# A transformer block with 576 features: 64x64 tiles for the last 64 features of every projection, with biases moved off TensorE

## The chip, the cores and the metric

The kernel runs on one core of a Trainium2 chip. The metric is the device time of one execution in microseconds (us). All data is fp32.

## The reference, cut to what matters

Two batches of 2048 tokens with C = 576 features go through one conditioned transformer block: 16 heads of D = 36 features, and an MLP with FF = 2304.

```python
ada = silu(c) @ W_ada + b_ada          # six vectors of 576 for each batch
h = layernorm(x) * (1 + scale_msa) + shift_msa
qkv = h @ W_qkv + b_qkv                # 576 -> 1728
o = softmax((q * D**-0.5) @ k.T) @ v   # for each head
x = x + gate_msa * (o @ W_proj + b_proj)
h = layernorm(x) * (1 + scale_mlp) + shift_mlp
x = x + gate_mlp * (gelu(h @ W_fc1 + b_fc1) @ W_fc2 + b_fc2)
```

## The kernel before, in words

A projection sums over 576 features in KC = 5 chunks: four of P = 128 partitions and one of KL = 64. In the last chunk a 65th row holds the bias in the weights and a one in the activations, so the bias is added by the matmul. Only the first layer of the MLP (`up_to`, lines 990 to 1047) differs: it takes the last 64 features of two column blocks together, in four matmuls of 64x64 (`last`, line 992, matmul line 998; a "quad" below), with features held twice, in partitions 0 to 63 and 64 to 127. Its bias is added by ACT (line 1023).

*Front* (lines 159 to 484). For four token blocks of QB = 512 of batch 0, `queries_keys_values` normalises, turns (L218) and modulates tokens (L136, L138) and computes queries and keys (L233, nine column blocks m) and values (L258, four tiles of tokens, two halves of C2 = 288 columns). The results go to DRAM (`qk_d`, `v_d`). Beside this, `later` computes the conditioning (`rows_of`, L331, into PSUM cleared by `cleared`, L313) and multiplies W_proj and W_fc2 by their gates (`gated`). Two PSUM pools serve: three `wide` tiles of two banks, and two single `bank`s.

*Main part* (from line 487). There are 128 units, 8 blocks of 512 queries times 16 heads. Each unit has NG = 4 groups, and one pass of the loop over G handles, in the order of the code: scores of a later group on PE (L538, 36x64 tiles) and their copy by ACT (L551); a step of other work from `fill`; exponentials by ACT (L597); at a unit's first group the turn of the maxima (`turn`, L574); the last part of the fill step (`lasts`); values weighted by exponentials (`weigh`, L609, 64x64 tiles); running maxima (L556) and the subtraction of the maximum (L593) on DVE; then `take`, which copies a unit's sum out of PSUM (L621, L622); then `flush`, which runs what an earlier step put into `later`; then the second half of the fill step, `dones`, which empties its PSUM; and `advance`, which moves the loads of the next item by one step.

The fill steps are generators. First come queries, keys and values of batch 1 (`projections`, L812 and L774), then for each finished block k an item `[gather(k), block(k), k]`. `gather` loads the block's sums and outputs, inverts the sums, and multiplies (L867 to L901); the reciprocals go through DRAM (`rec_d`, stored from POOL, and loaded by 20 DMAs on SP). `block` calls `begin` for the output projection (po, L929), the residual and the statistics, then runs the MLP: pf (L1012, L998), gelu on ACT and DVE, py (L1062), in three parts (`down`). A block's last part runs behind `begin` of the next block, when that is ready.

The order is set by a planner written out by hand: each step yields a cost, `RATE` is credited in each pass, and a step runs in each even pass, and in an odd one when the credit is above `RATE`. Odd passes otherwise turn two pieces of normalised tokens (`lights`, L719). POOL's queue carries weights, x, `gather`'s loads and the accumulating stores of the second half of each head (L630); SP's carries keys, values, the maxima (`m_d`, L585 and L588) and `r`. Each of these queues is worked in program order, so a DMA that waits holds those behind it. What remains behind the loop (the end of block 6 and all of block 7's MLP) runs without attention beside it, and `room` then takes PSUM from two pools.

Of the kernel before, what the change touches and what calls it, by code (L numbers as in the profile page):

```python
# [22 lines left out]
def dit_block_kernel(  # L23
# [51 lines left out]
    wpr_d = [scratch.tile([C + 1, C], F32, name=f"wpr_d{b}") for b in range(B)]  # L75
    w2_d = [scratch.tile([FF, C], F32, name=f"w2_d{b}") for b in range(B)]
    gb_d = [scratch.tile([C], F32, name=f"gb_d{b}") for b in range(B)]
    NB = B * NQB
# [12 lines left out]


    mod = const.tile([P, 4, KC, B], F32, name="mod")
    nc.vector.memset(mod, 0.0)
    nc.vector.memset(mod[KL : KL + 1, 0:2, KC - 1, :], 1.0)
    b1 = const.tile([P, NF], F32, name="b1")
# [59 lines left out]
    with ExitStack() as front:  # L156
# [32 lines left out]
        def queries_keys_values(b, tb):  # L189
# [11 lines left out]
            for i in range(TB):  # L201
                xn = lnp.tile([P, CP], F32, tag="xn", name=f"xn_{b}_{tb}_{i}", bufs=6)
                seq(nc.vector.memset(xn[:, C:CP], 0.0))
                seq(
                    nc.vector.tensor_scalar(
                        xn[:, 0:C], xts[i], rs[:, i : i + 1], nm[:, i : i + 1],
                        op0=ALU.mult, op1=ALU.add,
                    )
                )
                xns.append(xn)  # L210
# [4 lines left out]
            def turn(kc):  # L215
                pt = bank(f"pt_{b}_{tb}_{kc}")
                for i in range(TB):
                    seq(nc.tensor.transpose(pt[:, ts(i, P)], xns[i][:, ts(kc, P)], ident))  # L218
                return pt

            pts = []
            if (b, tb) == (0, 0):
                pts = [turn(kc) for kc in range(2)]
                yield
# [4 lines left out]
            for m in range(2 * C // P):  # L229
                pq = bank(f"pq_{b}_{tb}_{m}")  # L230
                for kc in range(KC):
                    seq(
                        nc.tensor.matmul(  # L233
                            pq,
                            lhsT=w_in[: rows(kc), kc, ts(m, P)],
                            rhs=hT[: rows(kc), kc, :],
                            start=(kc == 0),
                            stop=(kc == KC - 1),
                        )
                    )  # L240
                ev = evp.tile([P, QB], F32, tag="ev", name=f"ev_{b}_{tb}_{m}")
                if m < C // P:
                    seq(nc.scalar.mul(ev, pq, SCALE))
                elif m == C // P:
                    seq(nc.vector.tensor_scalar_mul(ev, pq, qscale))
                else:
                    seq(nc.vector.tensor_copy(ev, pq))
                seq(nc.sync.dma_start(out=qk_d[b][ts(m, P), ts(tb, QB)], in_=ev))
                if m == 2 * C // P - 1 and tb == NQB - 1:
                    first_keys.extend(load_keys(0))  # L250
                yield
            for i in range(TB):
                t = tb * TB + i
                pv = wide(f"pv_{b}_{t}")
                for n in range(2):
                    for kc in range(KC):
                        seq(
                            nc.tensor.matmul(  # L258
                                pv[:, n, :C2],
                                lhsT=hT[: rows(kc), kc, ts(i, P)],  # L260
                                rhs=w_in[: rows(kc), kc, ds(2 * C + n * C2, C2)],
                                start=(kc == 0),
                                stop=(kc == KC - 1),
                            )
                        )
                vt = evp.tile([P, H, HA], F32, tag="vt", name=f"vt_{b}_{t}", bufs=3)
                seq(nc.vector.memset(vt[:, :, 0:1], 1.0))
                to = vt.rearrange("p (n h) e -> p n h e", n=2)
                for n in range(2):
                    src = pv[:, n, :C2].rearrange("p (h d) -> p h d", d=D)  # L270
                    if i % 2:
                        seq(nc.scalar.copy(to[:, n, :, 1:HA], src))
                    else:
                        seq(nc.vector.tensor_copy(to[:, n, :, 1:HA], src))
# [4 lines left out]
        hTs = {}  # L279
        stages = [queries_keys_values(0, tb) for tb in range(NQB)] + [queries_keys_values(1, 0)]  # L280
# [5 lines left out]
        def load_in(n):  # L286
# [4 lines left out]
            seq(nc.sync.dma_start(out=to[0:KL, KC - 1, :], in_=last[:, cols]))  # L291
            seq(nc.sync.dma_start(out=to[KL : KL + 1, KC - 1, :], in_=b_qkv[cols].unsqueeze(0)))

        load_in(0)
        load_in(1)
        next(stages[1])
        load_in(2)

# [23 lines left out]
        seq(nc.vector.tensor_copy(cT.rearrange("p k b -> p (k b)"), pt[:, 0 : KC * B]))  # L322
        def rows_of(part):
# [19 lines left out]
        def modulation(part, t):  # L343

            pm = wide(f"pm_{part}")[:, 0, :]
# [9 lines left out]
            spans = [(0, P, 0, KC - 1), (0, KL, KC - 1, KC)]  # L355
            if part // 3:
                spans.append((64, KL, KC - 1, KC))
# [59 lines left out]
        def later():  # L417
# [5 lines left out]
            yield  # L423
            yield
            g1 = []
            yield from gates(2, g1)
            was[3] = load_ada(3)
            g2 = []
# [3 lines left out]
            for b in range(B):  # L432
                seq(nc.vector.tensor_scalar_mul(half[b], g2[b], 0.5))
                r = ap.tile([1, C], F32, name=f"b2_{b}")
                seq(nc.gpsimd.dma_start(out=r, in_=b_fc2.unsqueeze(0)))
                seq(nc.vector.tensor_mul(r, r, g2[b][0:1, :]))
                seq(nc.gpsimd.dma_start(out=gb_d[b].unsqueeze(0), in_=r))
# [7 lines left out]
                for i, job in enumerate(split(w_proj))  # L445
            ]
            jobs.append(
                (
                    b_proj.unsqueeze(0).unsqueeze(1), 1, 1, g1,
                    [wpr_d[b][C : C + 1].unsqueeze(1) for b in range(B)],  # L450
                )
            )
# [6 lines left out]
            for part in (3, 4):  # L459
                t = rows_of(part)  # L460
                yield
                modulation(part, t)
# [21 lines left out]
        seq(nc.gpsimd.dma_start(out=b1, in_=b_fc1.rearrange("(f p) -> p f", p=P)))  # L484
# [4 lines left out]
    with ExitStack() as main_part:  # L489
# [144 lines left out]
        state = {"wpr": None, "turn": 0}  # L634
# [15 lines left out]
        def load_cols(key, w, bias, lo, n):  # L650

            t = mp.tile([P, KC, 2 * P], F32, tag="w1", name=f"w1_{key}_{lo}")
            main, last = pieces(w)
            cols = ds(lo, n)
            seq(nc.gpsimd.dma_start(out=t[:, 0 : KC - 1, :n], in_=main[:, :, cols]))
            seq(nc.gpsimd.dma_start(out=t[0:KL, KC - 1, :n], in_=last[:, cols]))
            seq(
                nc.gpsimd.dma_start(out=t[KL : KL + 1, KC - 1, :n], in_=bias[cols].unsqueeze(0))
            )
            return t  # L660

        def load_square(key, src):

            if state["wpr"] is None or state["wpr"][0] != key:
                t = bp.tile([P, KC, C], F32, tag="wpr", name=f"wpr_{key}", bufs=1)
                rest, bias = src
                main = rest[0 : (KC - 1) * P].rearrange("(kc p) n -> p kc n", p=P)
                seq(nc.gpsimd.dma_start(out=t[:, 0 : KC - 1, :], in_=main))
                seq(nc.gpsimd.dma_start(out=t[0:KL, KC - 1, :], in_=rest[(KC - 1) * P : C]))
                seq(nc.gpsimd.dma_start(out=t[KL : KL + 1, KC - 1, :], in_=bias))  # L670
# [3 lines left out]
        def load_x(key, b, qb):  # L674
            xs = []
            for i in range(TB):
                t = bp.tile([P, C], F32, tag="x2", name=f"x2_{key}_{i}", bufs=8)
                seq(nc.gpsimd.dma_start(out=t, in_=x[b, ts(qb * TB + i, P), :]))
                xs.append(t)
            return xs  # L680

        def normed(key, xs, mvs, twice=False):
# [4 lines left out]
            def make(lo, hi):  # L687
                rs, nm = by
                for i in range(lo, hi):
                    xn = xp.tile([P, CP], F32, tag="xn", name=f"xn_{key}_{i}")  # L690
                    spans = [(0, 0, C)]
                    if twice:
                        spans.append((C, C - KL, KL))
                    else:
                        seq(nc.vector.memset(xn[:, C:CP], 0.0))
                    for to, at, n in spans:
# [8 lines left out]
            half = TB // 2  # L705
            return xns, [
                lambda: by.extend(rstd_of(bp, mvs, key)),
# [26 lines left out]
        made = {}  # L734

# [16 lines left out]
        def projections(b, tb):  # L752

            key = f"q{b}_{tb}"
            wv = load_square("v", (w_qkv[:, 2 * C :], b_qkv[2 * C :].unsqueeze(0)))
            pairs = [(m, min(2, 2 * C // P - m)) for m in range(0, 2 * C // P, 2)]
            ws = {m: load_cols(key, w_qkv, b_qkv, m * P, n * P) for m, n in pairs[:2]}
# [11 lines left out]
            def values(i):  # L769
                pv = room(f"pv_{key}_{i}")  # L770
                for n in range(2):
                    for kc in range(KC):
                        seq(
                            nc.tensor.matmul(  # L774
                                pv[n][:, :C2],
                                lhsT=hT[: rows(kc), kc, ts(i, P)],
                                rhs=wv[: rows(kc), kc, ts(n, C2)],
                                start=(kc == 0),
                                stop=(kc == KC - 1),
                            )  # L780
# [489 lines left out]
```

## Time and profile before

| | us |
|---|---|
| median of 3 runs | 3801.6 (3800.6 to 3804.5) |
| the profiled execution | 3804.53, its span 3802.8 |
| granted TensorE clock | 0.995 of full speed |
| front, to the first scores | 296.4 |
| main loop | 296.4 to about 3547 |
| behind the loop | from about 3547 |
| DMA | 362.6 MB, 95 GB/s over the span |

In the rows that follow, a row of the timeline has the start, the length, the engine and line, and how many records were merged; in square brackets stands the idle time before it and who ended it. A row of the waits has the engine and what it ran, after the arrow what it waited for, the sum, how often, and the longest. "PEld" is the weight load of PE.

### The profile page before, as it was taken

The page shows a single profiled execution, that of the slowest core. Times are in us where ns is not written, and L with a number is a line of the kernel's source. Part 1 is how long each engine was busy: PE and PEld are TensorE (multiplying, and loading weights), DVE is VectorE, ACT ScalarE, POOL GpSimd, SP SyncE. Part 2 cuts the span into 40 slices and gives each one's busy share as a digit, 9 for nine tenths or more (in the row PEclk, how much of TensorE's full clock was granted, in tenths as well). Part 3 has the DMA queues.
Part 4 walks back from the last instruction along what each step waited for, and adds up shares of the span by engine and source line. Part 5 has one row for each costly group of instructions (what it writes and reads, how often), then busy time and mean ns, then how long its engine had stood idle before and what let it go on. Part 6 is the DMA issues. An engine that isn't in the chain of part 4 may idle for free.

```text
span 3802.8 us, 58130 instructions
## 1 busy us (share of the span) xinstructions
PE 3748.3 (99%) x23429; PEld 1762.1 (46%) x23429; DVE 2946.1 (77%) x2995; ACT 2335.5 (61%) x2196; POOL 564.7 (15%) x814
## 2 busy tenths in 40 slices
PE   8999999999999999999999999999999999999998
PEld 4554343444344544444444544453444444444555
DVE  4525778788888888888889888888889888988422
ACT  0005667766866676667676677667666766776321
POOL 0201112111111021101111111012110211111111
PEclk9999999999999999999999999999999999999999
DMA  6722434344434344434343433434342444343321
GB/s 218 270 99 76 97 78 108 86 122 96 93 81 98 59 103 86 102 55 103 69 95 89 105 77 83 96 62 112 81 99 57 107 83 97 70 95 79 87 84 56
DMA packets 415986, 362.58 MB, mean 95 GB/s; under 512 B 312731, under 2 KB 312731, under 8 KB 415718
## 3 DMA queue, kind: packets, MB, share of 16 engines
q1 hardware_dynamic: 352662, 177.06, 23.5%
q0 software_dynamic: 61328, 178.27, 15.4%
q8 instruction: 185, 3.03, 0.4%
q10 hardware_dynamic: 1728, 3.54, 0.3%
q14 instruction: 83, 0.68, 0.1%
HBM read 287.52 MB, written 71.21 MB: 94 GB/s over the span
## 4 chain that ended last, share of the span: by engine, by line
PE 93%; issue 4%; DVE 1%; ACT 1%; DMA 1%; POOL 0%; POOLq 0%; SPq 0%; ACTq 0%; DVEq 0%
PE av L609 23%; PE s L538 23%; PE py L1062 13%; PE pf L1012 13%; PE pq_q L812 4%; PE pq L233 4%; PE po L929 4%; PE pv_q L774 2%; PE pf L998 2%; PE pv L258 2%; PE mt L574 2%; PE pa L331 0%; PE pt_b L719 0%; ACT e L551 0%; DMA o_d<-up 0%
## 5 line engine op out<-in xcount | busy, mean ns | idle before, releaser
L551 ACT COPY e<-s 128x1024 f32<-128x1024 f32 x1024 | 989.6, 1024 | 684.4 <-PE s L538 680.2
L593 DVE TENSOR_TENSOR e<-e,m 128x2048 f32<-128x2048 f32 x512 | 1161.6, 2274 | 3.2 <-DMA m<-m_d 3.2
L556 DVE TENSOR_TENSOR acc<-acc,e 128x1024 f32<-128x1024 f32 x768 | 938.9, 1222 | 197.6 <-ACT e L551 155.0
L597 ACT ACTIVATE e<-e 128x2048 f32<-128x2048 f32 x512 | 991.6, 1937 | 1.2 <-DVE e L593 1.1
L609 PE MATMUL av<-e,v 64*64 64x512 f32 x8192 | 981.7, 594 | 0.0
L538 PE MATMUL s<-qT,kT 36*64 36x512 f32 x8192 | 975.7, 590 | 3.1 <-ACT e L551 2.3
L1062 PE MATMUL py<-w,gT 128*128 128x288 f32 x2304 | 583.5, 411 | 5.2 <-DVE gT L1042 3.5
L538 PEld LDWEIGHTS s<-qT,kT 36*64 36x64 f32 x8192 | 310.2, 133 | 563.8 <-issue 517.5
L1012 PE MATMUL pf<-h_b,w_b 128*128 128x512 f32 x1152 | 533.6, 607 | 4.4 <-DMA w_b<-in_L_cond_W_fc_dram 4.3
L609 PEld LDWEIGHTS av<-e,v 64*64 64x64 f32 x8192 | 291.8, 133 | 518.3 <-issue 478.5
L1062 PEld LDWEIGHTS py<-w,gT 128*128 128x128 f32 x2304 | 433.3, 191 | 183.7 <-issue 40.0
L630 POOL DMA_DIRECT2D o_d<-up x128 | 109.8, 858 | 2091.1 <-DMA o_d<-up 1117.4
L1012 PEld LDWEIGHTS pf<-h_b,w_b 128*128 128x128 f32 x1152 | 208.9, 190 | 324.6 <-issue 312.0
L584 DVE TENSOR_REDUCE mx<-mt 128x4 f32<-128x512 f32 x128 | 88.2, 689 | 197.3 <-PE mt L574 196.8
L1023 ACT ACTIVATE gT<-pf,b 128x512 f32<-128x512 f32 x144 | 99.0, 688 | 191.3 <-PE pf L998 136.6
L1034 DVE SCALAR_TENSOR_TENSOR th<-th,gT 128x1024 f32<-128x1024 f32 x72 | 88.0, 1222 | 104.0 <-ACT th L1032 104.0
L929 PE MATMUL po<-wpr_p,oT 128*128 128x288 f32 (+1 forms) x640 | 163.0, 410 | 0.1
L556 DVE TENSOR_TENSOR acc<-e 128x1024 f32<-128x1024 f32 x128 | 155.4, 1214 | 9.2 <-ACT e L551 9.2
L233 PE MATMUL pq<-hT,w_in 128*128 128x512 f32 (+1 forms) x360 | 158.6, 597 | 0.3 <-ACT hT L136 0.2
L1074 DVE TENSOR_TENSOR x_b<-py,x_b 128x288 f32<-128x288 f32 x192 | 81.4, 451 | 93.0 <-PE py L1062 93.0
L929 PEld LDWEIGHTS po<-wpr_p,oT 128*128 128x128 f32 (+1 forms) x640 | 119.2, 190 | 54.2 <-issue 11.0
L631 POOL DMA_DIRECT2D sum_d<-up x128 | 143.6, 1122 | 0.0
(142 smaller groups left out, 2275.1 us busy)
## 6 DMA issues: line engine op xcount, KB each, us to landing
w<-w_d POOLq DMA_DIRECT2D x72, 576.0 KB, 5.9
v<-v_d SPq DMA_DIRECT2D x128, 296.0 KB
kT<-qk_d SPq DMA_DIRECT2D x256, 144.0 KB
w_b<-in_L_cond_W_fc_dram POOLq DMA_DIRECT2D x72, 512.0 KB, 4.6
m<-m_d SPq DMA_DIRECT2D x128, 256.0 KB
qT<-qk_d SPq DMA_DIRECT2D x256, 72.0 KB
w_d<-wg POOLq DMA_DIRECT2D x12, 864.0 KB, 4.9
qk_d<-ev SPq DMA_DIRECT2D x36, 256.0 KB
```

Source lines behind the costliest of these rows:

```text
L233: nc.tensor.matmul(pq, lhsT=w_in[: rows(kc), kc, ts(m, P)], rhs=hT[: rows(kc), kc, :], start=(kc == 0), stop=(kc == KC - 1),)
L538: nc.tensor.matmul(s[ts(c, 64), i, :], lhsT=self.kT[at, ds((2 * g + j) * P + 64 * c, 64)], rhs=self.qT[at, :], start=True, stop=True,)
L551: seq(nc.scalar.copy(self.es[g][:, j], s))
L556: top = lambda out, x, y: seq(nc.vector.tensor_max(out, x, y))
L593: seq(nc.vector.tensor_sub(e, e, m))
L597: seq(nc.scalar.activation(e, e, AF.Exp))
L609: nc.tensor.matmul(self.av[ts(i, 64), r, :], lhsT=self.v[ts(r, 64), ds((c + i * (HALF // P)) * HA, 64)], rhs=e[ts(r, 64), j, i, :], start= ...
L631: seq(nc.gpsimd.dma_start(out=sums, in_=hi[0:1, :], accum_op=ALU.add))
L812: nc.tensor.matmul(pq, lhsT=w[: rows(kc), kc, ts(j, P)], rhs=hT[: rows(kc), kc, :], start=(kc == 0), stop=(kc == KC - 1),)
L929: nc.tensor.matmul(po[n][:, :C2], lhsT=oT[: rows(kc), kc, ts(i, P)], rhs=wpr[: rows(kc), kc, ts(n, C2)], start=(kc == 0), stop=(kc == KC - 1),
L1012: nc.tensor.matmul(pfs[j], lhsT=w1[:, kc, ts(j, P)], rhs=h2[:, kc, :], start=(kc == 0 and j == 0), stop=(kc == KC - 2 and j == 1),)
L1062: nc.tensor.matmul(py[n][:, :C2], lhsT=gTs[f - f % 2][:, f % 2, ts(i, P)], rhs=w2s[f - f % 2][:, f % 2, ts(n, C2)], start=(j == 0), stop=( ...
```

## The change

- All projections take the last 64 features in quads. The tails of weights and activations are held twice; ones and bias rows go.
- Biases: queries, keys and the MLP's first layer get theirs when ACT or DVE empties PSUM, from a tile `bias`, which is loaded by rows and transposed on PE. Values get theirs in an addition on DVE (before: copies by ACT, in the front half of them by DVE). The gated bias of the output projection is added by loading it as a broadcast into the residual's tiles and accumulating x on top by DMA; that of the second layer by four accumulating DMAs, in place of a load and four additions on DVE.
- `gather` loads the residuals (before: `begin`). The first weights of an item are loaded in the item in front (`early`).
- In the loop `take` runs behind `dones`; the first half of xn is put off by a pass when the statistics came in the same one; costs, `RATE` (2.55 to 2.51) and the first credit (-10 to -32) are new.
- In the front, PSUM for the conditioning is cleared a step earlier, the first block's five transposes run together, queries and keys use `wide`.
- The very last part of block 7 runs its first two tiles together, all but the last two chunks first; its stores go out in halves from SP.

```diff
+    def quads(outs, lefts, rights, starts):
+        for r in range(2):
+            for c in range(2):
+                seq(
+                    nc.tensor.matmul(
+                        outs[r][ts(c, 64), :],
+                        lhsT=lefts[r][:, ts(c, 64)],
+                        rhs=rights[r],
+                        start=starts[r],
+                        stop=not starts[r],
+                    )
+                )
+    def halves(t, kc):
+        return [t[ts(r, 64), kc, :] for r in range(2)]
...
             pts = []
             if (b, tb) == (0, 0):
+                spare = [wide(f"pt_{i}") for i in range(2)]
                 pts = [turn(kc) for kc in range(2)]
+                pts += [turn(2 + n, spare[0][:, n, :]) for n in range(2)]
+                pts.append(turn(4, spare[1][:, 0, :]))
...
+            for m in range(0, NQK, 2):
+                pq = wide(f"pq_{b}_{tb}_{m}")
...
+                    if two and r == 0:
+                        quads(
+                            [pq[:, i, :] for i in range(2)],
+                            [w_in[ts(i, 64), KC - 1, ts(m + i, P)] for i in range(2)],
+                            tail,
+                            (False, True),
+                        )
...
+                if i % 2 == 0:
+                    rest_of(i, pvs[0])
+                    rest_of(i + 1, pvs[1])
...
+    def by_square(outs, src, t, i):
+        w_, tail = square(t)
+        for n in range(2):
+            for kc in range(KC - 1):
+                seq(
+                    nc.tensor.matmul(
+                        outs[n][:, :C2],
+                        lhsT=src[:, kc, ts(i, P)],
+                        rhs=w_[:, kc, ts(n, C2)],
+                        start=(kc == 0),
+                        stop=False,
+                    )
+                )
+        return lambda: quads(
+            [o[:, :C2] for o in outs],
+            [half[:, ts(i, P)] for half in halves(src, KC - 1)],
+            tail,
+            (False, False),
+        )
-        def load_x(key, b, qb):
+        def load_x(key, b, qb, bias=None):
             xs = []
             for i in range(TB):
                 t = bp.tile([P, C], F32, tag="x2", name=f"x2_{key}_{i}", bufs=8)
-                seq(nc.gpsimd.dma_start(out=t, in_=x[b, ts(qb * TB + i, P), :]))
+                if bias is not None:
+                    seq(nc.gpsimd.dma_start(out=t, in_=bias.partition_broadcast(P)))
                 xs.append(t)
+            how = {} if bias is None else {"accum_op": ALU.add}
+            for i, t in enumerate(xs):
+                seq(nc.gpsimd.dma_start(out=t, in_=x[b, ts(qb * TB + i, P), :], **how))
             return xs
...
             for i in range(TB):
                 yield values(i)
+                to = f"q{b}_{tb + 1}"
+                if i == 0:
+                    early[to] = first_cols(to)
...
-            seq(nc.gpsimd.dma_start(out=oT[0:KL, KC - 1, :], in_=o_d[k][(KC - 1) * P : C]))
-            seq(nc.gpsimd.memset(oT[KL : KL + 1, KC - 1, :], 1.0))
+            for half in halves(oT, KC - 1):
+                seq(nc.gpsimd.dma_start(out=half, in_=o_d[k][(KC - 1) * P : C]))
+            b, qb = divmod(k, NQB)
+            loaded[k] = load_x(f"b{k}", b, qb, gp_d[b])
             yield
             yield
             seq(nc.vector.reciprocal(sums, sums))
...
-            gb = xp.tile([P, CP], F32, tag="xn", name=f"gb_{k}")[:, :C]
-            seq(nc.gpsimd.dma_start(out=gb, in_=gb_d[b].partition_broadcast(P)))
-            extra = [
-                lambda i=i: seq(nc.vector.tensor_add(x2s[i], x2s[i], gb)) for i in range(TB)
-            ]
+            for t in x2s:
+                seq(
+                    nc.gpsimd.dma_start(
+                        out=t, in_=gb_d[b].partition_broadcast(P), accum_op=ALU.add
+                    )
+                )
...
+                early[k + 1] = {f: load_w1(k + 1, f) for f in (0, 2)}
                 yield from begin(k + 1)
...
-                    if f is not None:
+                    if f is None:
+                        return
+                    if state["norm"] == state["slot"]:
+                        later.append(f)
+                    else:
                         f()
...
+                    for lo, hi in ((0, per - 2), (per - 2, per)):
+                        for i in range(at):
+                            weigh(i, pys[i], lo, hi)
+                    yield 11.88, lambda: [add(i, pys[i]) for i in range(at)]
...
-            if 0 <= G < NU * NG and g == NG - 1:
-                units[u].take()
             flush()
             for done in dones:
                 done()
+            if 0 <= G < NU * NG and g == NG - 1:
+                units[u].take()
             advance()
```

## The prediction

> **What bounds the kernel now.** I read the page's table of engines and the chain that ended last first:
>
> ```profile
> PE 3748.3 (99%) x23429; PEld 1762.1 (46%) x23429; DVE 2946.1 (77%) x2995; ACT 2335.5 (61%) x2196; POOL 564.7 (15%) x814
> PE 93%; issue 4%; DVE 1%; ACT 1%; DMA 1%; POOL 0%; POOLq 0%; SPq 0%; ACTq 0%; DVEq 0%
> ```
>
> PE's busy time alone proves little, because pipelined matmuls overlap, but the chain says the same: 93% of what set the end is PE. A matmul taken off PE should therefore shorten the kernel by its own time. Next come PE's waits, the only other time to be won:
>
> ```profile
> PE pq_q L812 <- DMA w_q<-in_L_cond_W_qkv_dram: 7.3, 1, 7.3
> PE pf L1012 <- DMA w_b<-in_L_cond_W_fc_dram: 4.3, 1, 4.3
> PE pa L331 <- issue: 4.3, 3, 1.6
> PE py L1062 <- DVE gT L1042: 3.5, 1, 3.5
> PE s L538 <- ACT e L551: 2.3, 1, 2.3
> PE py L1062 <- DVE x_b L1074: 1.6, 1, 1.6
> ```
>
> Last, PE's timeline, for prices. Each fp32 matmul is two records there (x10 is five matmuls). In the main loop, in the front, and behind the loop:
>
> ```profile
> 437.20 4.56 PE L812 MATMUL pq_q<-h_q,w_q 128*128 128x512 f32 x10
> 449.20 4.56 PE L812 MATMUL pq_q<-h_q,w_q 128*128 128x512 f32 x10
> ...
> 596.62 4.56 PE L812 MATMUL pq_q<-h_q,w_q 128*128 128x512 f32 x10
> 608.14 4.56 PE L812 MATMUL pq_q<-h_q,w_q 128*128 128x512 f32 x10
> ...
> 2310.44 3.70 PE L1012 MATMUL pf<-h_b,w_b 128*128 128x512 f32 x8
> 2322.43 3.70 PE L1012 MATMUL pf<-h_b,w_b 128*128 128x512 f32 x8
> 2333.10 3.70 PE L1012 MATMUL pf<-h_b,w_b 128*128 128x512 f32 x8
> ```
> ```profile
> 97.02 30.23 PE L233 MATMUL pq<-hT,w_in 128*128 128x512 f32 x70
> ```
> ```profile
> 3651.48 1.09 PE L998 MATMUL pf<-h_b,w_b 64*64 64x512 f32 x8
> 3652.50 7.13 PE L1012 MATMUL pf<-h_b,w_b 128*128 128x512 f32 x16
> 3659.56 1.09 PE L998 MATMUL pf<-h_b,w_b 64*64 64x512 f32 x8
> ```
>
> Full 512-column matmuls in a row cost 30.08/35 = 0.8595 us each (start to start); 288-column ones 19.43/40 = 0.4858 (line 258, x80). 512 against 288 gives 1.67 ns a column and no fixed part, so 256 columns cost 0.432.
>
> **Part 1: the tails leave PE.** pf (lines 1012 and 998) already has the new form, so it prices it.
> - *In the loop* two steps of queries/keys, with one turn of maxima between them, take 12.00 + 11.52 = 23.52 us. Two steps of pf, with one turn, take 11.99 + 10.67 = 22.66. The difference, 0.86, is two tail matmuls against one quad beside the 64x64 av tiles. So a quad costs 0.86 there, the array's ideal, and 0.485 at 288 columns.
> - *Between full tiles* (behind the loop) quad plus eight full matmuls repeat every 3659.56 - 3651.48 = 8.08 us, of which eight times 0.8595 is 6.88. A quad costs 1.20, or 0.86 plus 0.34 for going into small tiles and back.
>
> The Trainium skill speaks against small tiles here: "TensorEngine Tiling (Array Packing)", section "Tiling Modes", says that a change of tiling mode drains the array. The row in the loop shows no added drain, because av changes the mode there anyway; the row behind the loop does. Were the drain paid at all 64 new quads of the loop too, 64 x 0.34 = 22 us of the gain below would go. I take each row in its place.
>
> Sums. Loop, 4 token blocks: 16 pairs x 0.86 = 13.8; four single column blocks, where four times 0.86 + 0.86 becomes eight half matmuls + half a quad, save 0.43 each = 1.7; 16 value tiles and 28 output projections (blocks 0 to 6) lose two 288-column tails and gain one 288 quad: 44 x 0.485 = 21.3. Together 36.8. Front, 4 blocks, with the drain: pair 2 x 0.86 - 1.20 = 0.515, times 4; single 0.07; values, two quads per two tiles under one drain, 4 x 0.486 - 0.97 - 0.34 = 0.63, times 2: 3.4 a block, 13.6. Behind the loop, 4 output projections x 0.14 = 0.6. **PE: -51.0.**
>
> **Part 2: the waits.**
> - w_q at 422.79: weights of the next item are loaded during its predecessor's values. 7.30 of idle goes, and the stretched group (7.45 against 4.56) gives 2.9 more: -10.2. Next late would be the turned h_q, whose last transposes ended at 410, before PE went idle at 415.5: nothing.
> - w_b at 3644.98: the same, 4.34 + (6.57 - 3.70) = -7.2. Next late is h_b: transposes end at 3640.6, evictions take 0.78 each on ACT, and the first four are needed one by one at 0.86; no new wait.
> - py at 3772.9 waits 3.53 for the last gelu. The two tiles' first four matmuls per half (16 x 0.486 = 7.8 us) now come first and cover it: -3.5.
> - At 1715 scores wait 2.27 for ACT, which had been given the new xn right behind the statistics of the same step; the groups there stretch by 1.8 and 1.5 more. Deferring xn to the next step removes it: -5.5.
> - At 3190 py waits 1.57 for its banks: DVE freed them only after `take`, which sat idle for av. With `take` behind the evictions: -1.6. The price: the sum's copies are later, by evictions of 0.8 to 1.9 us, and the next unit's first av matmul queues behind them; there PE has 1.7 of scores and 3.5 to 6 of a step to do first. Nothing.
> - pa's three waits (1.54, 1.61, 1.19): PSUM is cleared a step earlier, -4.3. Banks of pq in front of transposes (0.8, DVE ev L247): -0.8, because pq moves to the wide buffers.
> - Start: all five transposes move ahead of the modulation matmuls (12 x 0.135 = 1.6 later mod) and save as much behind them: nothing. Bias transposes and their three DVE operations lie under the 6.2 us that PE is idle before pa at 11.36. Last store: halves from SP, perhaps -0.5.
>
> I worked the planner's credit through with both sets of costs: both give 24 steps in odd slots and both leave the loop at the same step (pf 13 of block 6), so nothing moves from loop to tail. Sum of waits: **-33.6**, and I allow **+4** for new ones (steps fall into other odd slots; values are freed by DVE before turned transposes).
>
> **Part 3: what is added elsewhere.** Values go from ACT (402 ns a half) to DVE (449 ns as a copy, 451 for an add from PSUM, line 1074). In the loop that is 32 x 0.45 = 14 us more DVE, but the gb additions, 32 x 0.751 = 24 us, leave it. The skill's "TensorEngine Tiling", section "Performance Considerations", would have both engines empty PSUM once tiles speed PE up. By it values on DVE alone are a step back; were each of the 16 in the loop late by its two adds, 0.9 us, 14 us would go. The row says 39.5 of 54 us of DVE are busy in the value stage at 531, so I take nothing; the evicted bank is already waited for by 0.55 from ACT.
> POOL: `gather` now issues two tails, four broadcasts of the bias and four accumulating loads of x ahead of the store of the reciprocals; four accumulating gb loads follow `lit`, and the first add that needs those is eight steps away. SP gets two more loads of 0.4 us per block. What is queued behind POOL's wait is the rival below. Early w1 loads wait for the same two buffers at most one step; then only stores of o_d follow them. ACT's bias operand costs 688 against 597 ns, 36 times, off the path.
>
> **Sum.** 3804.5 profiled - 51.0 - 33.6 + 4 = 3723.9. The median is 2.9 below the profiled run: **3721 us**.
>
> **Rivals.**
> *A, as summed* (0.74): 3704 (no drain in front: -10; no new waits: -4; and a little at the start) to 3738 (half the waits come back).
> *B, the waits only change place* (0.12): the last three groups, or w_q and w_b, are followed by others as long. Then PE's 51 remain and some 5 of waits: 3746. For: PE at 99% leaves other engines little slack. Against: each wait has a named cause that the edit takes away, with nothing late behind it.
> *C, quads of 288 or 256 columns run at the price of 512* (0.08): four weight loads (133 ns each by line 538's PEld row) might bound them. 64 + 20 such quads x 0.375 = 31 lost: 3750. Against: the 310 us of PEld busy for 8192 loads are 38 ns each, 152 per four, under the 243 ns of one pass of 288.
> *D, slower: the bias row ahead of the reciprocals* (0.06).
>
> ```profile
> gb<-gb_d POOLq DMA_DIRECT2D x8, 288.0 KB, 6.5
> ```
> ```profile
> 1168.06 0.57 POOL L881 DMA_DIRECT2D rec_d<-sums  x1 [0.42 <-DVE sums L880]
> 1172.37 1.96 SPq L892 DMA_DIRECT2D r<-rec_d  x4
> 1178.39 0.35 SPq L585 DMA_DIRECT2D m_d<-mx  x1
> ```
>
> An accumulating load must wait on POOL until its broadcast has landed (nearest row: 6.5 us for one). Issues of 0.8, the 6.5 and four of 1.08 put the reciprocals' store at about 1178.5 instead of 1168.1; r follows at 1182.5 on SP, and the next unit's maxima m_d, behind it on SP, slip by 6 us. m would land near 1190.4, and the subtraction that needs it runs at 1191.7; exponentials are a further step away, so some 5 us are spare. Each us beyond that stops PE, in each of seven blocks. If the four together need 6.5, nothing; the other end, four in series (26 us), is 19 later, 14 beyond the slack: 7 x 14 = 98, and 3819. It becomes slower than before when the broadcasts take over about 23 us. The 1024 KB of oT land in 6.1, so I take the short end. Partly so: 3757. Behind the loop the same delay meets 14.5 us of slack (oT done 3580.8, po at 3595.3).
>
> **How the numbers follow.** A 0.74, B 0.12, C 0.08, D 0.06. 3704 to 3750 holds A, B and most of C, some 0.85. A measurement of this kernel can tell 0.2%, 8 us, from no change; only D reaches that: faster 0.95, same 0.01, slower 0.04.
>
> **What would show it.** Right: PE busy near 3700 or less; no w_q, w_b or gT row in PE's waits; two steps of queries/keys in 22.66; an output projection's step 0.49 shorter; m_d rows behind r at each block, with no wait of DVE for m. Wrong: line 593 waiting for m beyond the 3.2 us of before (D); PE groups of 288 quads over 0.6 (C); new PE waits on DVE for values, or on ACT e (B).

## The result, and the profile after

The changed kernel takes 3772.4 us (median of 6 runs, 3765.4 to 3775.8) where the kernel before takes 3802.2: a ratio of 0.9919 (95% interval 0.9906 to 0.9931). It is faster, as forecast, but by 30 us instead of 81, and outside the range. Its profiled run is its fastest, 3765.4 with a span of 3763.6, so the trace shows less of the loss than the median has. Beside the experiments the kernel before took 3803.5 to 3805.4, so differences to the changed kernel are good to some 3 us.

The engines on the page after:

```profile
PE 3706.8 (98%) x23926; PEld 1727.1 (46%) x23926; DVE 2950.2 (78%) x3002; ACT 2331.1 (62%) x2164; POOL 617.1 (16%) x868
```

PE's busy time fell by 41.5 us and the span by 39.2, so PE idles no less than before (56.8 us, where it was 54.5). The largest new waits of PE are these:

```profile
PE s L625 <- DMA qT<-qk_d: 10.7, 5, 5.0
PE pq L277 <- ACT ev L261: 6.9, 8, 1.2
PE pf L104 <- DVE x_b L1207: 5.6, 1, 5.6
...
PE pv L104 <- DVE vt L342: 3.0, 1, 3.0
...
PE pq L277 <- DVE ev L263: 2.0, 2, 1.0
```

None of the six rows shown of before is left: w_q, w_b, pa behind "issue", gT, ACT e and the banks of py are gone. The first and the third of the new ones cost more than their idle time, because the groups of matmuls behind them are stretched as well.

The trace can be cut where the first scores start and where the last av ends. The gain of the profiled run is then: front 296.4 - 293.5 = 2.9 us; main loop 28.9; behind the loop 7.3.

*Front.* From the first pq to the first scores PE is busy 248.5 us instead of 262.0: 13.5 less, where 13.6 was forecast. But its idle time there went from 10.0 to 18.6, and the first pq starts at 26.4 instead of 24.4. From the timeline of DVE and PE:

```profile
93.38 0.75 DVE L525 TENSOR_TENSOR row<-row,gate 1x576 f32<-1x576 f32 x1 [2.62 <-DMA row<-in_L_cond_b_proj_dram]
95.02 1.24 PE L104 MATMUL pv<-w_in,hT 64*64 64x288 f32 x8 [3.02 <-DVE vt L342]
...
106.55 7.13 PE L277 MATMUL pq<-hT,w_in 128*128 128x512 f32 x16 [0.81 <-ACT ev L261]
113.61 1.09 PE L104 MATMUL pq<-hT,w_in 64*64 64x512 f32 x8
115.56 7.13 PE L277 MATMUL pq<-hT,w_in 128*128 128x512 f32 x16 [0.86 <-ACT ev L261]
```

A pair takes 115.56 - 106.55 = 9.01 us, against 8.60 (ten times 0.8595) in the old form. Of this, 0.86 is a wait until ACT has emptied the pair's first half; the other 8.15 are near the 8.08 of a quad and eight full matmuls behind the loop before. The first two rows are the 3.0 us of pv: DVE stands waiting for a bias row, with values to empty behind it.

*Main loop.* Two steps of queries/keys with one turn, and two output projections one pass apart:

```profile
463.84 3.70 PE L952 MATMUL pq_q<-h_q,w_q 128*128 128x512 f32 x8
474.98 3.70 PE L952 MATMUL pq_q<-h_q,w_q 128*128 128x512 f32 x8
486.50 3.70 PE L952 MATMUL pq_q<-h_q,w_q 128*128 128x512 f32 x8
...
1252.02 4.15 PE L776 MATMUL po<-wpr_p,oT 128*128 128x288 f32 x16
1260.18 4.15 PE L776 MATMUL po<-wpr_p,oT 128*128 128x288 f32 x16
```

The first three are 22.66 us from end to end, the price read from pf. A pass with an output projection takes 8.16; before, it was 8.65:

```profile
1256.49 5.12 PE L929 MATMUL po<-wpr_p,oT 128*128 128x288 f32 x20
1265.14 5.12 PE L929 MATMUL po<-wpr_p,oT 128*128 128x288 f32 x20
```

Taking the usual length of each kind of pass (its first quartile) and summing what passes took beyond it, 19.9 us were lost before and 30.6 after. So without such losses the loop gained 28.9 + 10.7 = 39.6, a little over the 36.8 of the sum. Of the 30.6, 27 lie in six passes, at blocks 0, 5 and 6: at each, the pass in which PE waits for the next unit's keys and queries (qT) and its neighbour. Block 0, in the timeline of POOL's and SP's DMA issues and of PE's scores:

```profile
740.75 0.57 POOL L1024 DMA_DIRECT2D sums<-sum_d  x1 [1.59 <-DMA sum_d<-up]
...
744.26 2.17 POOL L797 DMA_DIRECT2D x_b<-gp_d  x4
...
750.57 0.88 POOL L801 DMA_DIRECT2D x_b<-in_x_dram  x1 [4.13 <-DMA x_b<-gp_d]
...
755.93 0.85 POOL L801 DMA_DIRECT2D x_b<-in_x_dram  x1 [0.66 <-DMA x_b<-gp_d]
757.04 0.87 POOL L1040 DMA_DIRECT2D rec_d<-sums  x1
...
763.44 1.48 SPq L1051 DMA_DIRECT2D r<-rec_d  x4
765.03 0.34 SPq L672 DMA_DIRECT2D m_d<-mx  x1
...
772.06 0.36 SPq L170 DMA_DIRECT2D qT<-qk_d  x1
...
775.06 1.97 PE L625 MATMUL s<-qT,kT 36*64 36x512 f32 x4 [4.96 <-DMA qT<-qk_d]
```

This is the chain of rival D. POOL waits for the broadcasts and stores the reciprocals 16.3 us behind its load of the sums (14.9 to 17.8 over the eight blocks; before, 2.8 to 6.5). SP waits for those, and the maxima and then the next unit's keys queue behind. PE had been ready for them since 770.1.

Only three of the seven blocks in the loop were hit. In all seven the last qT load goes out 29.5 to 32.1 us behind the load of the sums (before: 20.5 to 28.1). At blocks 0, 5 and 6 PE wants the keys 29.4 to 30.2 us behind that load, at the four others after 36: there the delay stays hidden.

*Behind the loop* w_b and gT are gone, but pf waits 5.6 us for DVE:

```profile
3551.56 0.69 DVE L1059 TENSOR_TENSOR oT<-oT,r 128x512 f32<-128x512 f32 x1 [14.84 <-DMA r<-rec_d]
...
3557.07 0.81 DVE L1207 TENSOR_TENSOR x_b<-py,x_b 128x288 f32<-128x288 f32 x2
3557.58 1.97 PE L104 MATMUL pf<-h_b,w_b 64*64 64x512 f32 x4 [5.65 <-DVE x_b L1207]
```

DVE stood still 14.84 us in front of its first product with r, with an addition that frees PSUM queued behind it: the same late reciprocals.

### The profile page after: what moved, and what is told of

It reads as the page before. It is cut to its first block, busy times and chain, and to the rows that moved or that the text cites. A ratio compares the mean times of both kernels' runs of the same rounds, so it can differ in the third digit from the quotient of the medians.

```text
span 3763.6 us, 59194 instructions
## 1 busy us (share of the span) xinstructions
PE 3706.8 (98%) x23926; PEld 1727.1 (46%) x23926; DVE 2950.2 (78%) x3002; ACT 2331.1 (62%) x2164; POOL 617.1 (16%) x868
## 5 line engine op out<-in xcount | busy, mean ns | idle before, releaser
L625 PE MATMUL s<-qT,kT 36*64 36x512 f32 x8192 | 984.2, 592 | 11.8 <-DMA qT<-qk_d 10.7
L1158 ACT ACTIVATE gT<-pf,bias 128x512 f32<-128x512 f32 x144 | 99.1, 688 | 204.6 <-PE pf L104 134.6
L277 PE MATMUL pq<-hT,w_in 128*128 128x512 f32 (+1 forms) x320 | 130.6, 560 | 10.6 <-ACT ev L261 6.9
L776 PE MATMUL po<-wpr_p,oT 128*128 128x288 f32 x512 | 132.6, 412 | 0.0
L743 POOL DMA_DIRECT2D w_b<-in_L_cond_W_fc_dram x72 | 68.3, 949 | 299.6 <-PE pf L1147 269.7
```

The lines of the kernel that those rows point to most:

```text
L277: nc.tensor.matmul(pq[:, r, :n], lhsT=w_in[:, kc, cols], rhs=hT[:, kc, at], start=(kc == 0 and not (two and r)), stop=(kc == KC - 2 and tw ...
L625: nc.tensor.matmul(s[ts(c, 64), i, :], lhsT=self.kT[at, ds((2 * g + j) * P + 64 * c, 64)], rhs=self.qT[at, :], start=True, stop=True,)
L776: nc.tensor.matmul(outs[n][:, :C2], lhsT=src[:, kc, ts(i, P)], rhs=w_[:, kc, ts(n, C2)], start=(kc == 0), stop=False,)
```

## The experiments

Each ran beside the kernel before; ratios are to that.

**e1: the residual loads behind the store of the reciprocals.**

```diff
-            b, qb = divmod(k, NQB)
-            loaded[k] = load_x(f"b{k}", b, qb, gp_d[b])
             yield
             yield
             seq(nc.vector.reciprocal(sums, sums))
             seq(nc.gpsimd.dma_start(out=flat_rows(rec_d[k]), in_=sums))
+            b, qb = divmod(k, NQB)
+            loaded[k] = load_x(f"b{k}", b, qb, gp_d[b])
```

> Theory: the changed kernel lost most of its expected gain because the residual loads in the gather hold POOL's queue until the bias broadcasts have landed, so the reciprocals are stored late, their loads hold SP, and the next unit's keys and maxima come late. Moving the residual loads (broadcasts and accumulating loads) behind the store of the reciprocals should then remove PE's waits for qT (10.7 us idle, 27 us with the stretched groups) and the wait of 5.6 us behind the loop: 30 to 42 us faster than the changed kernel, about 3735 us. Rival: the added DMA traffic itself makes the reciprocals and keys late, wherever it is issued: then it stays within 10 us of the changed kernel.

Measured: 3738.9 us (3737.8 to 3741.2), ratio 0.9829 (0.9816 to 0.9842), 33.5 us below the changed kernel. In PE's waits the row of pf behind the loop is gone and that of qT is short:

```profile
PE s L625 <- DMA qT<-qk_d: 2.4, 2, 1.6
```

SP's own waits for the reciprocals are 135.8 us over the eight blocks, where the changed kernel had 227.0 and the kernel before 114.9. With the same loads at another place in the queue most of the loss is gone, so its main cause is the order on POOL and not the DMA traffic. Not all of it: at block 0 the two passes still lose 7 us (11 in the changed kernel). There SP issued the load of the maxima 7.6 us behind their store, while the residual loads were in flight (changed kernel 3.5, before 6.1), and the keys waited for it to land. Whether that is the traffic was not tested.

**e2: both halves of a pair are emptied behind the second half's matmuls.**

```diff
                     if two:
-                        kept(m + r, pq[:, r, :])
+                        if r == 1:
+                            for i in range(2):
+                                kept(m + i, pq[:, i, :])
                         yield
```

> Theory: in the front, the matmuls of the second half of a wide PSUM tile wait for the emptying of its first half because that is issued ahead of them and belongs to the same tile. With both halves emptied behind the second half's matmuls, the ten waits of PE for ev (8.9 us) vanish: 9 us faster than the changed kernel. Rival: the wait is for buffers of ev or for the bank itself; then the waits only move and the time stays within 3 us.

Measured: 3764.0 us (3758.1 to 3765.0), ratio 0.9890 (0.9877 to 0.9904), 8.4 below the changed kernel. No row of pq waiting for ev is left, and the first scores start at 282.9 us, where in the changed kernel, e1, e3 and e9 they start at 292.3 to 297.6. The order of the code makes the wait: whether by the bookkeeping of one tile or by something in PSUM is not told apart. That the medians differ by nearly the 8.9 us of the waits is in part luck. The gather is that of the changed kernel, and this profiled run lost some 8 us more to it in the loop, so that the two profiled runs are only 0.8 apart:

```profile
PE s L627 <- DMA qT<-qk_d: 16.5, 3, 6.3
```

**e3: broadcasts in front, accumulating loads behind the reciprocals.**

```diff
-            for i, t in enumerate(xs):
-                seq(nc.gpsimd.dma_start(out=t, in_=x[b, ts(qb * TB + i, P), :], **how))
+            if bias is None:
+                add_x(xs, b, qb)
             return xs
...
             seq(nc.gpsimd.dma_start(out=flat_rows(rec_d[k]), in_=sums))
+            add_x(loaded[k], b, qb, accum_op=ALU.add)
```

> The broadcasts stay in front of the reciprocals, only the four accumulating loads of x go behind them. Theory (POOL is held by the wait for the broadcasts to land): as fast as with all loads behind, within 5 us, because four issues of some 0.6 us are all that is left in front. Rival (the traffic of the broadcasts in flight slows the reciprocals' way through DRAM): clearly slower than with all loads behind, by 10 us or more.

Measured: 3745.0 us (3740.6 to 3746.6), ratio 0.9842 (0.9828 to 0.9855): 27 us of the 33 come back, 6 do not. The two expectations named 5 and 10 as their marks, and it lies between, nearer to the first. POOL's wait for the broadcasts is the main cost; the broadcasts being ahead leaves a smaller one, and whether by their issues or their traffic is open. SP waits 183 us for the reciprocals, between 136 and 227.

**e4: e1 and e2 together, and the products of the gated bias rows on GpSimd.** In the front, DVE stood waiting for the DMAs of those rows with values to empty behind them (pv's 3.0 us).

```diff
-                    seq(nc.vector.tensor_mul(r, r, g[b][0:1, :]))
+                    seq(nc.gpsimd.tensor_mul(r, r, g[b][0:1, :]))
```

> All residual loads behind the reciprocals, both halves emptied late, and the four small products of the gated bias rows on GpSimd in place of DVE, so that DVE does not stand waiting for their DMAs while values wait in PSUM. Theory: the gains add: about 35 and 9, and 3 for the wait of pv for DVE in the front: some 47 us faster than the changed kernel, about 3725 us. Rival: the waits overlap in part, and it is no better than the better of the single ones.

Measured: 3724.3 us (3723.4 to 3726.1), ratio 0.9790 (0.9776 to 0.9803), 48.1 below the changed kernel. The gains add: 33.5 + 8.4 leave 6 for the third edit and chance. pv's row is gone. One wait for qT is left, 2.7 us at block 0, where the two passes lose 9. This version beats both kernels and lies 3 us from the forecast made for the changed one, with three edits that the forecast did not have.

The next four undo one part each in e4, to see whether the parts that should remove waits do.

**e5: take ahead of dones**, as before.

```diff
+            if 0 <= G < NU * NG and g == NG - 1:
+                units[u].take()
             flush()
             for done in dones:
                 done()
-            if 0 <= G < NU * NG and g == NG - 1:
-                units[u].take()
```

> Base for this and the next three: the mended kernel (residual loads behind the reciprocals, both halves emptied late, bias rows on GpSimd), 3724 us. Here take runs ahead of dones again. Theory of the prediction: two py steps now fall on a unit's last pass in an odd slot, each would wait 1.6 us for its banks as the one of before did: some 3 us slower, with rows of py waiting for DVE x_b. Rival: the order of take does not matter in this schedule: the same within 1 us and no such rows.

Measured: 3728.5 us (3724.7 to 3732.0), ratio 0.9799 (0.9784 to 0.9813); its runs overlap those of e4, so times do not tell them apart. The waits do:

```profile
PE po L778 <- DVE x_b L1086: 3.3, 2, 1.7
PE py L1197 <- DVE x_b L1209: 3.1, 2, 1.6
```

The two py steps wait the 1.6 each that was expected, and two po steps, which had been overlooked, do too. With the stretched groups these four passes lose 9.9 us; the profiled run hides most of it, because it lost 4 us less at block 0 and its front ended 2.7 us earlier.

**e6: xn is never put off.**

```diff
-                    if state["norm"] == state["slot"]:
-                        later.append(f)
-                    else:
-                        f()
+                    f()
```

> The first half of xn is not put off when the statistics came in the same pass. Theory: in this schedule one block has its last po and first py in neighbouring passes (block 1) and another runs py in an odd slot behind them: 5.5 us slower, with scores waiting for ACT, as at 1715 us of before. Rival: the other schedule alone has moved the collision away: the same within 1 us.

Measured: 3726.8 us (3725.4 to 3729.7), ratio 0.9795 (0.9781 to 0.9810), again not told from e4 by time. One collision comes back, at block 1, and costs 4.2 us over two passes (2.5 and 1.7), less than the 5.5 counted at 1715:

```profile
PE s L627 <- ACT e L640: 2.3, 1, 2.3
```

**e7: no weights in the item in front.**

```diff
-                if i == 0:
-                    early[to] = first_cols(to)
...
-                early[k + 1] = {f: load_w1(k + 1, f) for f in (0, 2)}
```

> No weights are loaded in the item in front. Theory: both waits of before return, 10.2 us for w_q in the loop and 7.2 us for w_b behind it: 17 us slower, about 3741 us. Rival: the residual loads, which have left begin, already let the weights of the next block go earlier on POOL: then only the first returns, 10 us.

Measured: 3737.9 us (3736.4 to 3739.3), ratio 0.9823 (0.9807 to 0.9839): 13.6 slower than e4. Both waits return, the one in the loop with 9.95 us in its pass and the other with 4.34 of idle:

```profile
399.04 3.75 PE L954 MATMUL pq_q<-h_q,w_q 128*128 128x512 f32 x4 [7.50 <-DVE e L682]
399.19 1.07 POOL L803 DMA_DIRECT2D x_q<-in_x_dram  x2 [0.32 <-DMA w_q<-in_L_cond_W_qkv_dram]
...
3588.98 5.14 PE L1147 MATMUL pf<-h_b,w_b 128*128 128x512 f32 x8 [4.34 <-DMA w_b<-in_L_cond_W_fc_dram]
```

PE's first row names DVE as the one that ended the wait, but the weights landed at the same time: POOL, which waited for w_q too, goes on at 399.19. At the second, the group is stretched less than before (5.14 against 6.57 where 3.70 is usual). 10 + 4.3 + 1.4, less the 1.5 by which this run's front ended earlier, is near the 13.6.

**e8: the last part tile by tile.**

```diff
-                if part == NT3 - 1 and k == NB - 1:
+                if False:
```

> The last part of block 7 runs tile by tile again. Theory: the wait of py for the last gelu returns: 3.5 us slower, one row of py waiting for DVE gT. Rival: the wait is covered otherwise: no such row, the same time.

Measured: 3726.2 us (3725.0 to 3727.2), ratio 0.9793 (0.9778 to 0.9807). The wait is back, with exactly its old length:

```profile
PE py L1197 <- DVE gT L1177: 3.5, 1, 3.5
```

The profiled spans of e8 and e4 are the same (3723.2 and 3722.9), because e8's front happened to end 5.1 us earlier with the same code; the median lost 1.9. The row proves the 3.5, the time does not.

**e9: the loads of r on POOL's queue, in the changed kernel.**

```diff
-                                nc.sync.dma_start(
+                                nc.gpsimd.dma_start(
                                     out=r[ds(to + f - kc * P, n), :],
```

> The changed kernel, residual loads where it has them, but the loads of the reciprocals r issued from POOL in place of SP. Theory (second link: SP is held by r, and keys and maxima queue behind it): the reciprocals stay as late, but PE's waits for qT vanish from the loop, some 27 to 34 us faster than the changed kernel's 3772, with the wait behind the loop still there, longer by the slower issues of POOL (22 of them). Rival (keys are late because the DMA engines are full, not because SP is held): the waits for qT stay.

Measured: 3762.0 us (3760.6 to 3764.2), ratio 0.9888 (0.9873 to 0.9903), 10 us below the changed kernel instead of 27. The waits for qT are gone from the loop, so SP being held is what made keys late. But others came:

```profile
PE mt L661 <- DVE acc L643: 8.8, 2, 8.0
PE py L1195 <- DVE x_b L1207: 8.6, 2, 5.1
```

Why DVE is late stands in its groups: 40 products with r, with 69.3 us of idle in front of them (changed kernel 42.2, before none):

```profile
L1059 DVE TENSOR_TENSOR oT<-oT,r 128x512 f32<-128x512 f32 x40 | 27.5, 686 | 69.3 <-DMA r<-rec_d 69.3
```

DVE works in order too, and a product that waits for r holds the maxima and the additions behind it. Whatever queue r takes, late reciprocals reach PE.

**e10: the same edit in e4.**

> The mended kernel (3724 us) with r from POOL too. Theory: its one remaining wait for qT, at the first block (2.7 us idle, 9 us with the stretched pass), goes: 5 to 9 us faster, about 3717. Rival: 22 slower issues on POOL hold weights and stores, and new waits take the place: 3725 or more.

Measured: 3733.5 us (3728.7 to 3735.8), ratio 0.9811 (0.9795 to 0.9828), 9 us slower than e4. The time is the rival's: PE waits 9.8 us for DVE's maxima in front of the turn instead of 2.7 for qT. Its reason holds in part. POOL's queue shows what makes r late:

```profile
732.84 0.55 POOL L1040 DMA_DIRECT2D rec_d<-sums  x1
...
745.01 0.85 POOL L803 DMA_DIRECT2D x_b<-in_x_dram  x1 [1.01 <-DMA x_b<-gp_d]
745.55 2.43 POOL L1053 DMA_DIRECT2D r<-rec_d  x4
```

The loads of r now stand behind the accumulating loads, 12.7 us behind the store of the reciprocals, and DVE waits 54.9 us for them where it waited 12.7 in e4. Early reciprocals and r on SP are the better pair.

## Why the prediction was wrong, point by point

**The tails leaving PE: right, in mechanism and size.** 13.5 against 13.6 in the front; 39.6 against 36.8 in the loop, with the prices of 0.86 and 0.485 found in the passes themselves. The 0.34 us that the prediction took for the change of tiling mode was paid between full tiles in the front (8.15 a pair) and not beside av. Rival C fell, by the 8.16 of a pass. Its own sign was badly chosen: quads of 288 columns run as groups of 0.71 us, over its mark of 0.6, but those of 512 take 1.09 for a price of 0.86, so a group's length has some 0.23 on top of the price. C's sum also counted the 16 quads of 512 columns in the loop, which could not lose.

**The waits removed: right, with small errors of size.** All six rows are gone. Undone one by one: w_q 10 as counted; w_b nearer 6 than 7.2; gT 3.5; xn 4.2 instead of 5.5; take 9.9 in the new schedule, where e5's expectation had 3 and the prediction, for the old one, 1.6. So rival B did not come true: the new waits come from what the change moved, not from what lay behind the old ones.

**The front's banks: wrong sign.** "Because pq moves to the wide buffers" was booked as -0.8. The transposes' wait for banks did go, but in the wide buffers the second half of a pair waited for the emptying of the first, +8.9. The code showed it: `kept` stands in the loop over r, ahead of the next matmuls into the same tile. That the step read "wide" as more room, and did not walk through the order of one pair, is the failing.

**Values on DVE alone: right in the loop, wrong in the front.** Turned tokens waited 0.15 us each instead of 0.55. In the front pv lost 3.0, because DVE's small products wait for DMAs there, four now where two were.

**The failing step was rival D's price.** The chain was named link by link, and given 0.06 and no time. Two things were wrong.

First, the delay. D's own terms, 0.8 + 6.5 + 4 x 1.08 = 11.6, were entered as 10.4 (1178.5 - 1168.1), and four broadcasts together need more than 6.5: at block 0 the last accumulating load went out 11.7 us after the first broadcast (755.93 - 744.26). Behind it POOL had a further store at block 0, and three loads of weights at the later ones, ahead of the reciprocals. So r starts 21.1 to 23.3 us behind the load of the sums, where D had 17.3 and the kernel before 7.1 to 10.6.

Second, the slack, and this weighs more. D measured it for m only. The sign that it gave, DVE waiting for m, did come up, but small: 8.6 us against 3.2 (the other row is its wait for r, where it had none before).

```profile
DVE oT L1059 <- DMA r<-rec_d: 42.2, 11, 14.8
...
DVE e L680 <- DMA m<-m_d: 8.6, 8, 3.5
```

What stopped PE were the keys, which SP issues behind m and the next part of r, and their slack differs from block to block. D looked at block 1, where in the kernel before the last qT load went out 9.6 us ahead of the scores that needed it; at block 0 it was 5.5. At blocks 5 and 6 it had been over 10, but after the change PE wants the keys there some 6 and 9 us sooner behind the load of the sums. At 770.1 PE wanted keys that were issued from 771.7. Behind the loop, D set the late reciprocals against po's slack of 14.5 us, and not against the additions that stand behind the products on DVE.

The chain cost 27 us in the loop of the fastest run (20 of them gone in e1, the other 7 at block 0), some 7 more behind it, and in the median still more: e1 gave back 33.5.

In sum: 3723.9 was forecast for a profiled run, of which +4 for new waits. Measured were 27 and 7 for the chain, 9 for the halves, 3 for pv and 2 for the start, 48 in all: 44 more, less some 3 that the loop gained beyond its sum. The run took 41.5 more.

The start of the front is open. The first pq came 2 us later, 1.65 of it idle for which the profile names no cause; and over e4 to e8, with one front, the first scores started anywhere between 275.5 and 280.6 us.

## What to carry to other kernels

When loads move to an earlier place, follow each queue they pass: not only what the moved loads wait for, but what is behind them on that queue, and what is behind *that* on the next one, down to the operand with the least time between issue and use. A DMA that must wait for another DMA belongs behind everything in its queue that others are waiting for. In a queue worked in order, one late product or load holds unrelated ones, so moving it to another queue mostly changes who is late (e9, e10). And slack is a matter of the schedule: one block does not show that of the others.

## What the runs showed that was not expected

A broadcast of 288 KB alone in its place landed in 6.5 us in the median before; of the 32 that go out in fours, the landing took from 1.5 to 9.7 us, 6.9 in the median, and it is the last of the four that counts. The front moved by up to 5 us between runs of identical code, which is more than three of the edits were worth: there, rows of waits decide and times do not.
